# Expert weights of a routed feed-forward layer: rank comparison in 16 bit by quarters, one factor applied on ScalarE, heads summed on GpSimd

## The chip, the cores and the metric

The kernel runs on one core of a Trainium2 chip. The metric is the device time of one execution in microseconds; a kernel is judged by the median of its runs. The engines are named as in the profile: PE (TensorE; PEld is its weight load), DVE (VectorE), ACT (ScalarE), POOL (GpSimd), SP (the queue that issues DMAs).

## The reference, cut to what matters

One transformer layer on `x[8, 512, 256]`: `x + attention(layernorm(x)) + ffn(layernorm(x))`. Attention has 16 heads of width 16 and three branches (compressed, selected blocks, local window). The feed-forward part adds a dense gated layer and a lookup of experts by product keys:

```python
sim = jnp.einsum('btphn,hkpn->pbthk', q, keys)      # p: x or y half, 4 heads, 64 keys
sc, ix = jax.lax.top_k(sim, 8)
all_sc = sc[0][..., :, None] + sc[1][..., None, :]   # 8 x 8 pairs per head
scores, pk = jax.lax.top_k(all_sc.reshape(b, t, 4, 64), 8)
idx = take(ix[0] * 64 + ix[1], pk)                   # expert = x * 64 + y
w = silu(einsum('btd,bthkd->bthk', hidden, down_embed[idx])) * softmax(scores)
experts_states = einsum('bthk,bthkd->btd', w, up_embed[idx])
mlp = silu(h @ Wg + bg) * (h @ Wu + bu) @ Wd + bd
```

There are 1024 experts, so x counts in 16 places (NX = 16) and y in 64 (NK = 64). For every token the kernel needs a dense row of 1024 weights: for each head the softmax weight of a chosen pair (x, y), zero elsewhere, summed over the four heads (PH = 4).

## The kernel before, in words

The 4096 tokens are 32 tiles of 128 tokens (partitions); four tiles make a batch row. For each tile a set of generator functions does one stage each: `queries`, `logits`, `select`, `compressed`, `weights`, `products` and `finish` are attention, `choose_experts`, `route` and `experts` are the product-key lookup, `hidden` (for two tiles at a time) is the dense layer, and `project` multiplies by the up embeddings and the output weights and stores. Nearly all matmuls have f32 operands.

The order on each engine is written at build time by a planner, the class `Conductor`. A stage yields the engine and the buffers that it needs next; the planner keeps a clock for each engine, adds a cost for every recorded instruction (`FIXED` plus `EACH` per element in `book`, with extra terms), and lets the stage go on that can start first, by rank where two are within `NEAR`. Each engine then executes its instructions strictly in that order, waiting on semaphores. So an instruction that is late holds up all that stand behind it on its engine. `Stock` objects are sets of buffers: two pairs of PSUM banks for attention scores (`pairs`), four single banks (`banks`), two 128x1024 f32 buffers (`bigs`), two buffers for exponentiated scores (`wTs`). All instructions are recorded in one helper, so every row of the profile says L160, and rows are told apart by the tensors that they write and read.

The stages around the change:

- `choose_experts` (line 974) takes the top 8 of 64 keys for both halves and four heads, builds one-hot tables in 16 bit (`at_y` in one of the `bigs`, shown as `big<-cbf,ix`, and `at_x`), counts how many y each x keeps, and lets 16 matmuls on the one-hot tables put into one PSUM bank the rank of each y place less 8, and the number of y that each x place keeps. ACT copies these to `rc` (lines 1031 to 1034), head by head. `ed` holds exponentiated scores, 4 heads x (64 + 16), the x part divided by the softmax sum.
- `route` (line 1051) makes the row `gw` of 1024 weights. For each head DVE writes a 0/1 mask of 16 x 64 into a `big` buffer (rank + 8 < count, `big<-rc`), POOL multiplies it by y's factor and then by x's factor from `ed` (`big<-big,ed`), and adds it to `gw` (`gw<-gw,big`; for the first head the second product goes to `gw` itself).
- `experts` (line 1080) multiplies tokens by the down embeddings, applies silu in two steps (ACT writes a tanh to `aT`, DVE combines), transposes `gw` on PE, and multiplies.

The other uses of ACT are copies out of PSUM (`acs`, `qx`, `lg`, `q`, `attnT` and others), exponentials of attention scores (`wT`), and two activations for each of eight steps of `hidden` (`xg`, and one in place in PSUM), which take a bias column by pointer.

Of the kernel before, what the change touches and what calls it, by code (L numbers as in the profile page):

```python
# [9 lines left out]
BF16 = mybir.dt.bfloat16  # L10
U32 = mybir.dt.uint32
AF = mybir.ActivationFunctionType
ALU = mybir.AluOpType
# [3 lines left out]
P = 128  # L17
# [9 lines left out]
NEXP = 1024  # L27
NK = 64
PH = 4
KPH = 8  # L30
NX = NEXP // NK
# [10 lines left out]
_BF_COLS = [  # L42
    ("identb", P), ("win", P + WIN), ("caus", P), ("causT", P), ("bandT", P), ("prevT", WIN),
    ("cmask", NT * NB), ("oneh", 2 * G),
    ("ytab", NK * PH), ("ranks", KPH * P),
]


# [12 lines left out]
def shape_constants():  # L61

    p = np.arange(P)[:, None]
    q = np.arange(P)[None]
    c = np.zeros((P, NCONST), np.float32)
    m = np.zeros((P, NBF), np.float32)

    def put(name, v):
        a, b = _OFF[name]
        c[:, a:b] = v  # L70

    def putb(name, v):
        a, b = _BOFF[name]
        m[:, a:b] = v

    put("ident", np.eye(P))
    put("any", p >= G)
    put("grp", p // 32 == np.arange(4)[None])
    put("head4", p // NB == np.arange(H)[None] % 4)

    putb("identb", np.eye(P))
    back = p + WIN - np.arange(P + WIN)[None]
    putb("win", np.where((back >= 0) & (back <= WIN), 0.0, OUT))
    putb("caus", np.where(q <= p, 0.0, OUT))
    putb("causT", np.where(p <= q, 0.0, OUT))
    putb("bandT", np.where((q - p >= 0) & (q - p <= WIN), 0.0, OUT))
    putb("prevT", np.where(np.arange(WIN)[None] <= p % WIN, 0.0, OUT))

    pos = P * np.arange(NT)[None, :, None] + p[:, :, None]
    n = np.arange(NB)[None, None]  # L90
    low = -(1.0 + n / 128.0) * 2.0 ** 100
    putb("cmask", np.where(pos >= (n + 1) * G, 0.0, low).reshape(P, -1))
    r = np.arange(2 * G)[None]
    putb("oneh", r % G == NT * 2 * (r // G) + p // G)
    putb("ytab", np.arange(NK * PH)[None] // PH)
    putb("ranks", np.concatenate([(j - KPH) * np.eye(P) for j in range(KPH)], 1))
    return c, m.astype(ml_dtypes.bfloat16)


def bc(ap, axis, n):  # L100
    a = ap.unsqueeze(axis)
    shape = list(a.shape)
    shape[axis] = n
    return a.to_broadcast(shape)
# [59 lines left out]
class Conductor:  # L164
# [19 lines left out]
    def book(self, eng, op, args, kw):  # L184
        aps = [a for a in [*args, *kw.values()] if hasattr(a, "shape")]
        n = max(int(np.prod(a.shape[1:])) for a in aps)
        if eng == "PE":
            if op == "transpose":
                cost = 0.11
            else:  # L190
                n = int(np.prod(args[2].shape[1:]))
                cost = (n * 0.42e-3 if args[2].dtype == BF16 else max(n, 32) * 1.68e-3) / self.share
        elif eng == "SP":
            cost = 0.06
        else:
            each = self.EACH[eng]
            if eng == "DVE" and all(a.dtype == BF16 for a in aps):
                each /= 2
            cost = self.FIXED[eng] + each * n
            if op in ("match_replace", "max_index", "tensor_tensor_reduce"):  # L200
                cost += 0.08
        j = self.cur
        start = max(self.at[eng], j.end + (self.HOP[j.eng] if eng != j.eng else 0.0))
        if eng == "POOL" or eng == "DVE" and op in ("tensor_tensor", "scalar_tensor_tensor") and not any(
                a.tensor is self.psum.tensor for a in aps):

            s, e = self.port["DVE" if eng == "POOL" else "POOL"]
            if s <= start:
                start = max(start, e)
            self.port[eng] = (start, start + cost)  # L210
        self.at[eng] = start + cost
        self.busy[eng] += cost
        j.end, j.eng = start + cost, eng
# [41 lines left out]
def tile_kernel(ctx, tc, x, wq, wk, wqT, wv, wo, wck, wcv, wga, bga, wgu, bg, bu, wd, bd,  # L255
# [5 lines left out]
    pe, vec, act, pool, sp = (Engine(con, e, n) for e, n in (  # L261
        (nc.tensor, "PE"), (nc.vector, "DVE"), (nc.scalar, "ACT"), (nc.gpsimd, "POOL"),
        (nc.sync, "SP")))
    mm = pe.matmul
# [3 lines left out]
    def buf(name, shape, dt=F32):  # L268
        return cp.tile(shape, dt, name=name, tag=name)

    def stock(name, n, shape, dt=F32):
        return Stock(con, [buf(f"{name}{i}", shape, dt) for i in range(n)])
# [26 lines left out]
    def const(name):  # L299
        a, b = _OFF[name]  # L300
        return cst[:, a:b]

    def bconst(name, rows=slice(0, P)):
        a, b = _BOFF[name]
        return cbf[rows, a:b]

    ident, identb = const("ident"), bconst("identb")
    cmask = bconst("cmask").rearrange("p (i n) -> p i n", n=NB)
    ytab = bconst("ytab").rearrange("p (y h) -> p y h", h=PH)
# [8 lines left out]
    bigs = stock("big", 2, [P, NEXP])  # L318
# [87 lines left out]
    cnt, et = buf("cnt", [P, KPH, PH], BF16), buf("et", [P, 2 * PH, KPH])  # L406
    past, rz = buf("past", [P, PH, KPH]), buf("rz", [P, PH])
    eds = stock("ed", 2, [P, PH, NK + NX])
    rcs = stock("rc", 2, [P, PH * (NK + NX)])
    lasts = stock("last", 2, [P, 1])  # L410
    gws = stock("gw", 1, [P, NEXP])
    aTs = stock("aT", 2, [P, 8, P])
# [14 lines left out]
    for m in range(2):  # L427
        pfh = banks.take()
        for c in range(4):
            mm(pfh.ap[:, c * P:(c + 1) * P], wpqT_s[:, c, m * P:(m + 1) * P], keys_s[:, c, :],  # L430
               start=True, stop=True)
# [6 lines left out]
    PE, DVE, ACT, POOL, SP = "PE", "DVE", "ACT", "POOL", "SP"  # L438
# [535 lines left out]
    def choose_experts(t):  # L974
# [4 lines left out]
        for kc in range(2):  # L979
            mm(pt.ap, t.row.xnT.ap[:, kc, i * P:(i + 1) * P], wf_s[:, kc, :], start=kc == 0,  # L980
               stop=kc == 1)
# [8 lines left out]
        ed = t.ed.ap  # L990
# [31 lines left out]
        pr = pt.ap[:, :PH * (NK + NX)]  # L1022
        for j in range(KPH):
            rank = bconst("ranks")[:, j * P:(j + 1) * P]
            mm(pr[:, :PH * NK], rank, at_y[:, j].rearrange("p y h -> p (y h)"),
               start=j == 0, stop=False, skip_group_check=True)
        for j in range(KPH):
            mm(pr[:, PH * NK:], identb, at_x[:, j].rearrange("p x h -> p (x h)"),
               start=False, stop=j == KPH - 1, skip_group_check=True)
        ayh.free()  # L1030
        yield ACT,
        for lo, n in ((0, NK), (PH * NK, NX)):
            act.copy(t.rc.ap[:, lo:lo + PH * n].rearrange("p (h y) -> p h y", y=n),
                     pr[:, lo:lo + PH * n].rearrange("p (y h) -> p h y", y=n))
        pt.free()
        yield DVE,
        vec.tensor_tensor(sums, bc(et[:, :PH, :], 3, KPH), bc(et[:, PH:, :], 2, KPH), ALU.mult)
# [13 lines left out]
    def route(t):  # L1051

        yield None, t.ev("r")
        ed = t.ed.ap
        ry = t.rc.ap[:, :PH * NK].rearrange("p (h y) -> p h y", y=NK)
        cx = t.rc.ap[:, PH * NK:].rearrange("p (h x) -> p h x", x=NX)
        for h in range(PH):
            mh = yield DVE, bigs
            m = mh.ap.rearrange("p (x y) -> p x y", y=NK)
            vec.scalar_tensor_tensor(m, bc(ry[:, h, :], 1, NX), float(KPH), bc(cx[:, h, :], 2, NK),  # L1060
                                     ALU.add, ALU.is_lt)
            yield POOL,
            pool.tensor_tensor(m, m, bc(ed[:, h, :NK], 1, NX), ALU.mult)
            exb = bc(ed[:, h, NK:], 2, NK)
            if h == 0:
                t.gw = yield POOL, gws
                g3 = t.gw.ap.rearrange("p (x y) -> p x y", y=NK)
                pool.tensor_tensor(g3, m, exb, ALU.mult)
            else:
                yield POOL,  # L1070
                pool.tensor_tensor(m, m, exb, ALU.mult)
                yield POOL,
                pool.tensor_tensor(g3, g3, m, ALU.add)
            mh.free()
        pool.tensor_tensor(t.gw.ap[:, NEXP - 1:], t.gw.ap[:, NEXP - 1:], t.last.ap, ALU.add)
        for x_ in (t.ed, t.rc, t.last):
            x_.free()
        t.done("gw")
# [112 lines left out]
    for jp in range(2):  # L1191
        each(tiles, lambda t: t.n + 0.24, finish(jp))
    each(tiles, lambda t: t.n + 0.15, choose_experts)
    each(tiles, lambda t: t.n + 0.2, route)
    each(tiles, lambda t: t.n + 0.5, experts)
    each(halves, lambda h: 2 * h.n, fetch)
# [52 lines left out]
```

## Time and profile before

| | |
|---|---|
| median of 3 runs | 1878.66 us (1877.88 to 1882.4) |
| profiled execution | 1871.73 us, span 1869.9 us |
| mean granted TensorE clock | 0.969 |
| PE busy | 1696.6 us, 91% of the span |
| PEld busy | 1271.4 us, 68% |
| DVE busy | 1479.3 us, 79% |
| ACT busy | 692.6 us, 37% |
| POOL busy | 1022.6 us, 55% |
| DMA | 56.11 MB, mean 30 GB/s |

Busy time is the part of the span in which an engine had an instruction in work; a wait for a shared resource within an instruction counts as busy, a wait for a semaphore does not. The chain of waits follows the last instruction back to what released each step; its shares say which engine's work stood one behind the other.

### The profile page before, as it was taken

The numbers are of one execution on the slowest core, as the hardware profiler recorded it, in microseconds if no ns is written. First come the engines' busy times: TensorE is split into PE (matmuls) and PEld (weight loads), VectorE is DVE, ScalarE is ACT, GpSimd is POOL, SyncE is SP. The second block draws the span as 40 slices with busy tenths as digits, with TensorE's granted clock in tenths as the row PEclk, the third lists the DMA queues.
The fourth block names the chain that finished last, engine by engine and source line by source line (L and its number), as shares of the span: only waits on it lengthen the run. The fifth ranks groups of instructions, "written<-read, shape, count | busy, mean of one in ns | idle before, by whom it ended". The sixth has DMA issues, their size and how long they took to land.

```text
span 1869.9 us, 47619 instructions
## 1 busy us (share of the span) xinstructions
PE 1696.6 (91%) x19208; PEld 1271.4 (68%) x19208; DVE 1479.3 (79%) x5292; ACT 692.6 (37%) x1370; POOL 1022.6 (55%) x789
## 2 busy tenths in 40 slices
PE   3899989999989988899899998989989899998989
PEld 2677666777667766677677765766757677676657
DVE  2688896978879789768879878688786877969982
ACT  1353424424345232443334432334324333343233
POOL 2156647454766356556355562755546556474663
PEclk9999989999999999999899999999999999998999
DMA  5011100111001100010000110001000010100000
GB/s 175 10 42 25 30 18 13 36 36 32 24 24 37 25 20 28 24 42 25 18 26 28 42 32 18 13 25 42 25 24 24 20 36 25 30 19 18 30 24 18
DMA packets 55068, 56.11 MB, mean 30 GB/s; under 512 B 21696, under 2 KB 38080, under 8 KB 54848
## 3 DMA queue, kind: packets, MB, share of 16 engines
q1 hardware_dynamic: 54848, 53.07, 9.9%
q8 instruction: 151, 2.47, 0.6%
q14 instruction: 69, 0.57, 0.1%
HBM read 48.02 MB, written 4.19 MB: 28 GB/s over the span
## 4 chain that ended last, share of the span: by engine, by line
PE 61%; DVE 30%; issue 3%; ACT 2%; POOL 1%; SPq 1%; DMA 1%; DVEq 0%; ACTq 0%; POOLq 0%
PE psum L160 61%; DVE bm L160 4%; DVE big L160 3%; DVE mr L160 2%; DVE ixu L160 2%; DVE pick L160 2%; DVE ml L160 1%; DVE aT L160 1%; DVE at_x L160 1%; DVE sums L160 1%; ACT wT L160 1%; DVE top L160 1%; SPq L160 1%; DVE junk L160 1%; DVE hT L160 1%
## 5 line engine op out<-in xcount | busy, mean ns | idle before, releaser
L160 POOL TENSOR_TENSOR big<-big,ed 128x1024 f32<-128x1024 f32 x224 | 488.6, 2181 | 427.5 <-DVE big L160 387.9
L160 ACT ACTIVATE wT<-psum 128x1024 f32<-128x1024 f32 x224 | 219.3, 1023 | 167.4 <-PE psum L160 167.2
L160 PE MATMUL psum<-xnT,wb 128*128 128x256 f32 x1024 | 256.2, 395 | 22.6 <-DVE aT L160 13.7
L160 DVE TENSOR_REDUCE bm<-psum 128x32 f32<-128x512 f32 (+2 forms) x224 | 200.3, 912 | 69.8 <-PE psum L160 69.6
L160 PEld LDWEIGHTS psum<-xnT,wb 128*128 128x128 f32 x1024 | 193.1, 196 | 59.7 <-DVE aT L160 14.5
L160 POOL TENSOR_TENSOR gw<-gw,big 128x1024 f32<-128x1024 f32 x96 | 229.6, 2392 | 6.7
L160 PE MATMUL psum<-k,q 32*128 32x384 f32 (+3 forms) x1024 | 186.5, 469 | 1.6 <-DVE ml L160 1.6
L160 DVE SCALAR_TENSOR_TENSOR big<-rc 128x1024 f32<-128x1024 f32 x128 | 166.2, 1298 | 5.8 <-POOL gw L160 3.7
L160 PE MATMUL psum<-qx,k 32*128 32x128 f32 (+1 forms) x4352 | 152.4, 271 | 11.8 <-DVE ml L160 9.9
L160 PEld LDWEIGHTS psum<-qx,k 32*128 32x128 f32 (+1 forms) x4352 | 125.9, 174 | 48.9 <-issue 29.8
L160 PE MATMUL psum<-wT,v 128*32 128x128 f32 x3584 | 138.7, 280 | 16.6 <-ACT wT L160 15.7
L160 PEld LDWEIGHTS psum<-wT,v 128*32 128x32 f32 x3584 | 87.3, 110 | 80.7 <-ACT wT L160 37.0
L160 PE MATMUL psum<-xnT,deT_s 128*128 128x128 f32 x1024 | 135.5, 289 | 4.3 <-DVE yo L160 1.8
L160 PEld LDWEIGHTS psum<-xnT,deT_s 128*128 128x128 f32 x1024 | 128.6, 203 | 15.0 <-issue 2.7
L160 PE MATMUL psum<-wd_s,hT 128*128 128x256 f32 x512 | 124.8, 389 | 4.9 <-DVE hT L160 4.2
L160 DVE SCALAR_TENSOR_TENSOR aT<-aT,psum 128x512 f32<-128x512 f32 x128 | 87.1, 681 | 49.5 <-ACT aT L160 34.0
L160 ACT ACTIVATE xg<-psum,bgh 128x256 f32<-128x256 f32 x128 | 61.0, 477 | 164.8 <-PE psum L160 164.3
L160 PE MATMUL psum<-ue_s,aT 128*128 128x256 f32 x512 | 119.5, 384 | 2.1 <-DVE aT L160 1.7
L160 PEld LDWEIGHTS psum<-wd_s,hT 128*128 128x128 f32 x512 | 94.9, 193 | 22.5 <-DVE hT L160 5.1
L160 PEld LDWEIGHTS psum<-ue_s,aT 128*128 128x128 f32 x512 | 94.6, 190 | 18.7 <-DVE aT L160 1.9
L160 PEld LDWEIGHTS psum<-k,q 32*128 32x128 f32 x1024 | 76.0, 185 | 42.9 <-issue 32.7
L160 DVE SCALAR_TENSOR_TENSOR xg<-psum,xg 128x256 f32<-128x256 f32 x128 | 53.5, 418 | 59.9 <-ACT psum L160 59.6
(161 smaller groups left out, 3185.2 us busy)
## 6 DMA issues: line engine op xcount, KB each, us to landing
wb<-in_wgu SPq DMA_DIRECT2D x128, 256.0 KB, 2.6
xl<-in_x SPq DMA_DIRECT2D x8, 512.0 KB, 4.0
yo<-in_x SPq DMA_DIRECT2D x32, 128.0 KB, 2.1
out<-yo SPq DMA_DIRECT2D x32, 128.0 KB, 1.7
vl<-v SPq DMA_DIRECT2D x96, 8.5 KB, 1.8
deT_s<-in_deT SPq DMA_DIRECT2D x1, 1024.0 KB, 5.2
wd_s<-in_wd SPq DMA_DIRECT2D x1, 1024.0 KB, 7.7
ue_s<-in_ue SPq DMA_DIRECT2D x1, 1024.0 KB, 10.1
```

Source lines behind the costliest of these rows:

```text
L160: return f(*a, **k)
```

## The change

The masks of the four heads of a tile are no longer made head by head. They are made in four quarters of the x places, each quarter for all heads: 4 x places, 64 y places and 4 heads, again 1024 elements. DVE compares in 16 bit into a new buffer `chosen` (two of them). ACT then multiplies by x's factor: for each head and each x place of the quarter one activation of 64 elements, which takes the factor as its scale by pointer from `ed` and writes f32 to a `big` buffer. POOL multiplies the quarter by y's factor, adds the upper two heads to the lower two (512 elements), and adds the remaining two into the quarter of `gw` (256 elements). `rc` becomes 16 bit and keeps the order of PSUM, so ACT copies it in one piece; the 8 that the comparison used to add is now subtracted from the counts by one more matmul of 64 columns. The planner adds 0.09 to the cost of an activation with a scale or bias by pointer.

```diff
@@ _BF_COLS, shape_constants
-    ("ytab", NK * PH), ("ranks", KPH * P),
+    ("ytab", NK * PH), ("ranks", KPH * P), ("less8", 1),
...
+    putb("less8", -float(KPH))
@@ Conductor.book
+            if op == "activation" and any(hasattr(kw.get(k), "shape") for k in ("scale", "bias")):
+                cost += 0.09
@@ buffers
-    rcs = stock("rc", 2, [P, PH * (NK + NX)])
+    rcs = stock("rc", 2, [P, PH * (NK + NX)], BF16)
+    chosens = stock("chosen", 2, [P, NEXP], BF16)
@@ choose_experts
             mm(pr[:, PH * NK:], identb, at_x[:, j].rearrange("p x h -> p (x h)"),
-               start=False, stop=j == KPH - 1, skip_group_check=True)
+               start=False, stop=False, skip_group_check=True)
+        mm(pr[:, PH * NK:], identb, bconst("less8").to_broadcast([P, PH * NX]),
+           start=False, stop=True, skip_group_check=True)
         ayh.free()
         yield ACT,
-        for lo, n in ((0, NK), (PH * NK, NX)):
-            act.copy(t.rc.ap[:, lo:lo + PH * n].rearrange("p (h y) -> p h y", y=n),
-                     pr[:, lo:lo + PH * n].rearrange("p (y h) -> p h y", y=n))
+        act.copy(t.rc.ap, pr)
@@ route
-        ry = t.rc.ap[:, :PH * NK].rearrange("p (h y) -> p h y", y=NK)
-        cx = t.rc.ap[:, PH * NK:].rearrange("p (h x) -> p h x", x=NX)
-        for h in range(PH):
-            mh = yield DVE, bigs
-            m = mh.ap.rearrange("p (x y) -> p x y", y=NK)
-            vec.scalar_tensor_tensor(m, bc(ry[:, h, :], 1, NX), float(KPH), bc(cx[:, h, :], 2, NK),
-                                     ALU.add, ALU.is_lt)
+        ry = t.rc.ap[:, :PH * NK].rearrange("p (y h) -> p y h", h=PH)
+        cx = t.rc.ap[:, PH * NK:].rearrange("p (x h) -> p x h", h=PH)
+        t.gw = yield None, gws
+        XC = NX // 4
+        for c in range(4):
+            xs = slice(c * XC, (c + 1) * XC)
+            ch = yield DVE, chosens
+            cho = ch.ap.rearrange("p (x y h) -> p x y h", x=XC, h=PH)
+            vec.tensor_tensor(cho, bc(ry, 1, XC), bc(cx[:, xs, :], 2, NK), ALU.is_lt)
+            mh = yield None, bigs
+            m = mh.ap.rearrange("p (h x y) -> p h x y", h=PH, x=XC)
+            for h in range(PH):
+                if h % 2 == 0:
+                    yield ACT,
+                for x_ in range(XC):
+                    act.activation(m[:, h, x_, :], cho[:, x_, :, h], AF.Copy,
+                                   scale=ed[:, h, NK + c * XC + x_:NK + c * XC + x_ + 1])
+            ch.free()
             yield POOL,
-            pool.tensor_tensor(m, m, bc(ed[:, h, :NK], 1, NX), ALU.mult)
-            exb = bc(ed[:, h, NK:], 2, NK)
-            if h == 0:
-                t.gw = yield POOL, gws
-                g3 = t.gw.ap.rearrange("p (x y) -> p x y", y=NK)
-                pool.tensor_tensor(g3, m, exb, ALU.mult)
-            else:
-                yield POOL,
-                pool.tensor_tensor(m, m, exb, ALU.mult)
-                yield POOL,
-                pool.tensor_tensor(g3, g3, m, ALU.add)
+            pool.tensor_tensor(m, m, bc(ed[:, :, :NK], 2, XC), ALU.mult)
+            yield POOL,
+            half_ = m.rearrange("p h x y -> p h (x y)")
+            pool.tensor_tensor(half_[:, :2], half_[:, :2], half_[:, 2:], ALU.add)
+            pool.tensor_tensor(t.gw.ap[:, c * XC * NK:(c + 1) * XC * NK], half_[:, 0], half_[:, 1],
+                               ALU.add)
             mh.free()
```

## The prediction

> **What bounds the kernel now.** I began with the totals of the page and the chain of waits.
>
> ```profile
> PE 1696.6 (91%) x19208; PEld 1271.4 (68%) x19208; DVE 1479.3 (79%) x5292; ACT 692.6 (37%) x1370; POOL 1022.6 (55%) x789
> ...
> PE 61%; DVE 30%; issue 3%; ACT 2%; POOL 1%; SPq 1%; DMA 1%; DVEq 0%; ACTq 0%; POOLq 0%
> PE psum L160 61%; DVE bm L160 4%; DVE big L160 3%; DVE mr L160 2%; DVE ixu L160 2%; DVE pick L160 2%; DVE ml L160 1%; DVE aT L160 1%; DVE at_x L160 1%; DVE sums L160 1%; ACT wT L160 1%; DVE top L160 1%; SPq L160 1%; DVE junk L160 1%; DVE hT L160 1%
> ```
>
> PE is the largest, DVE second, and the end is set by both in turn. POOL, the engine that `route` loads most, holds 1% of the chain: its time matters only through what it does to others. The table of stretches of 25 us shows how the two take turns.
>
> ```profile
> 575.00:600.00 25.00, 23.47 (x325) 17.53 (x325) 23.63 (x111) 16.19 (x28) 17.36 (x12) 1.00 0.16 44
> 825.00:850.00 25.00, 25.00 (x135) 19.17 (x134) 22.79 (x122) 5.88 (x17) 8.16 (x11) 1.00 0.13 34
> 900.00:925.00 25.00, 18.15 (x130) 11.10 (x127) 23.65 (x97) 5.39 (x15) 8.41 (x10) 0.81 0.04 11
> ```
>
> The columns are PE, PEld, DVE, ACT and POOL busy, then the granted clock. From 825 us PE has no gap; from 900 us DVE is busy 23.65 of 25 us, PE idles 7 us and its clock is granted at 0.81. Relief of DVE can pay only in stretches of the second kind. The heaviest ACT stretch, from 575 us, already holds 16.19 us.
>
> A rule bears on how much there is to win. The Trainium skill (Perfetto Trace Analysis, Identifying the Most-Contended Engine) says that matmul busy time is a bad measure of headroom and weight-load busy time a good one. By that, PE at 68% would leave 32%, and freeing DVE could bring hundreds of us. But in the stretch without a PE gap PEld is at 19.17 of 25, 77%. Against that ceiling 68% is 0.89, so 11% is the most, and the totals of PE (91%) say 9%. I go by the trace.
>
> What PE waits for:
>
> ```profile
> PE psum L160 <- DVE aT L160: 24.5, 12, 5.9
> PE psum L160 <- DVE atc L160: 21.8, 10, 6.2
> PE psum L160 <- DVE hT L160: 17.4, 13, 3.1
> PE psum L160 <- ACT wT L160: 15.7, 24, 1.2
> ```
>
> (us in total, times, longest). DVE's waits are few and long, ACT's many and at most 1.2 us: ACT, idle 63% of the time, answers at once. The change touches exactly that.
>
> **DVE.** The removed and the nearest kept comparisons, as minimum/median/maximum in ns:
>
> ```profile
> L160 DVE SCALAR_TENSOR_TENSOR big<-rc x128: 1195/1216/2922, 87.9 to 1831.3; 128x1024 f32<-128x1024 f32 x128
> L160 DVE TENSOR_TENSOR big<-cbf,ix x32: 1212/1226/3247, 71.6 to 1764.7; 128x2048 bf16<-128x2048 bf16 x32
> L160 DVE TENSOR_TENSOR at_x<-cbf,ix x32: 411/420/2584, 72.8 to 1767.0; 128x512 bf16<-128x512 bf16 x32
> ```
>
> The last two have the form of the new comparison: 16 bit, a table repeated along one axis, innermost runs of 4 heads. Their medians give (1226 - 420) / 1536 = 0.525 ns an element, so 420 + 512 x 0.525 = 689 ns for 1024. The old one has a mean of 1298 ns, 82 above its median. How much waiting does the new one get? The skill (SBUF — State Buffer, Who interferes with whom) says that a DVE instruction with two SBUF inputs and a GpSimd instruction that reads SBUF exclude each other, and the later one waits for the whole of the other. Old and new both have two SBUF inputs, but the old one's row shows little of that, since POOL mostly stood waiting for it. The two 16-bit rows do show it: means of 1593 and 804 in the groups by shape, 367 and 384 above their medians. By the old row a new comparison is 771 ns and 128 of them save 67 us; by the rule, as those two rows price it, 1064 ns and 30 us. In the change ACT stands between DVE and POOL, so POOL is no longer idle by design when DVE compares, but its instructions are shorter: I take 250 ns of waiting, 939 ns, 359 saved, 46 us.
>
> POOL's part also frees DVE's other instructions. Mean less median, times 32, over the groups `at_y` (shown as `big<-cbf,ix`), `at_x` (2), `sums` (2), `pick`, `ix`, `et`, `ed`, `xn` is about 91 us of such waiting. The wait of a late comer goes with the square of the length of what it meets. The rows for POOL (busy us, mean ns of one, then idle time before):
>
> ```profile
> L160 POOL TENSOR_TENSOR big<-big,ed 128x1024 f32<-128x1024 f32 x224 | 488.6, 2181 | 427.5 <-DVE big L160 387.9 <-DVE gm L160 15.7 <-PE psum L160 7.2
> L160 POOL TENSOR_TENSOR gw<-gw,big 128x1024 f32<-128x1024 f32 x96 | 229.6, 2392 | 6.7
> ```
>
> A tile now has 7 x 2.18 + 1.99 + 3 x 2.39 = 24.4 us (squares 54); after it has 4 x (2.35 + 1.2 + 0.65) = 16.8 us (squares 30). The 2.35 is the median of `big<-big,ed`; 1.2 for 512 elements lies between half of `gw<-gw,big` and the 1.05 us of `ec`, 0.65 for 256 is near `ext<-mr,ms` (682 ns mean). Squares fall by 46%; with POOL's other work unchanged I take 40% of 91, 36 us; bounds 0 and 50. POOL itself loses 7.6 x 32 = 243 us.
>
> What of this lies on the path? DVE has 30% of 1869.9 = 561 us of its 1479 on the chain, 38%; `big` has 3%, 56 us of the 217 us of its two groups, 26%. So 46 x 0.26 + 36 x 0.38 = 26 us gained. Ends: 30 x 0.26 = 8, and (67 + 50) x 0.38 = 45. POOL's chain share, 19 us of 1023, makes its 243 us worth 4.
>
> **ACT.** 16 activations a quarter, 64 a tile, 2048 in all. None of them is in the trace; the nearest rows:
>
> ```profile
> L160 ACT ACTIVATE et<-et 128x64 f32<-128x64 f32 x32 | 8.2, 257 | 58.7 <-DVE et L160 58.6
> L160 ACT ACTIVATE xg<-psum,bgh 128x256 f32<-128x256 f32 x128 | 61.0, 477 | 164.8 <-PE psum L160 164.3
> ```
>
> ```profile
> 600.90 0.48 ACT L160 ACTIVATE xg<-psum,bgh 128x256 f32<-128x256 f32 x1 [1.14 <-PE psum L160]
> 601.27 0.44 ACT L160 ACTIVATE psum<-psum,bgh 128x256 f32<-128x256 f32 x1
> ...
> 619.44 0.37 ACT L160 COPY vtok<-psum 128x256 f32<-128x256 f32 x1 [0.18 <-PE psum L160]
> 619.71 0.38 ACT L160 COPY v<-psum 128x256 f32<-128x256 f32 x1
> ```
>
> Back to back, an instruction of 256 elements starts 0.37 us after one with a pointer, and 0.27 us after one without: 0.10 us for the pointer. `et` (64 elements, from SBUF) is followed after 0.16 us (618.65 to 618.81). So 0.26 us each: 4.2 us a quarter, 16.6 us a tile, 532 us in all. Ends: 0.16 (the pointer free), 328 us; 0.36 (no overlap), 737 us. The planner books 0.07 + 64 x 0.00083 + 0.09 = 0.213, so each batch of 16 runs 0.75 us longer than the order assumes. The one `rc` copy instead of two saves about 0.15 x 32 = 5 us.
>
> In the built order 112 batches have all 16 back to back and 32 have 8; `wT` stands directly behind 41 batches and `qx` behind 39, both in front of PE's attention matmuls; behind 21 it is `xg`, which feeds DVE. The cover of the batches is ACT's idle time; where PE or DVE needs the copy behind a batch, the cover is gone and up to 4.2 us show. A batch itself waits for a `chosen` and for POOL to free a `big`, and with it waits everything behind it on ACT. ACT's present work is on the chain for 37 of 693 us, 5.4%. At that share 532 us cost 29; for the copies that now come late behind batches I add 11: 40 us. Ends: 328 x 0.054 = 18, and 737 x 0.10 = 74.
>
> **PE** gets 32 matmuls of 64 columns, 0.05 to 0.2 us each by the row of `at_x` (13.3 us busy for 256; 197 ns each), at 61% on the chain 1 to 4 us: 2. No DMA is added; SP keeps its transfers.
>
> **Sum**, against the profiled span of 1869.9: -26 - 4 + 40 + 2 = +12, so 1882. The median of the runs stands 8.8 above the span, so about 1891, slower by 0.6%. Ends: -45 - 5 + 18 + 1 = -31 (1848) and -8 - 3 + 74 + 4 = +67 (1946).
>
> **Rivals.**
>
> *ACT hides, DVE's relief shows (faster).* The place is the stretches like 900 us, where DVE is full and ACT is at 5 of 25 us. If the batches lie there, they cost nearly nothing, about 10 us, and the freed DVE time counts at the mean share: 82 x 0.38 = 31. Then -31 - 4 + 10 = -25, about 1854. It decides where ACT's growth on the chain stays below the 30 us that DVE and POOL give, that is while ACT has less than about 3.6% of the chain. For it: ACT's idle 63%. Against it: the batches follow the comparisons, which are spread over all stretches. 34%.
>
> *ACT becomes the gate of attention (clearly slower).* Scores sit in two pairs of banks until `wT` is out; with 4.2 us in front, PE finds no free pair. If each of the 80 batches ahead of `wT` and `qx` costs 1 us: -30 + 80 + 2 = +52, about 1931. Against it: PE has the dense layer and the experts to go on with. 18%.
>
> *The comparison does not run at 16-bit speed*, so it stays near 1.2 us: DVE's 12 us fall away, +24, about 1903. The `at_x` row speaks against it. 5%.
>
> The small loss of the sum keeps 43%, and it reaches to no change and below. A difference of 0.3%, 5.6 us, is about what a measurement of this kernel can tell from none. From the cases: faster 0.34, within 0.3% 0.13, slower 0.53. The range 1844 to 1950 takes in the ends of the costs and the centres of the rivals.
>
> **What would show it.** DVE busy near 1400 us, POOL near 780, ACT near 1230 with 2048 rows `big<-chosen,ed` of about 0.35 us; `chosen<-rc` at a median of 0.69. If the sum is right, the chain shows ACT at 4 to 5% and DVE below 29%, and PE's waits for `wT` and `qx` rise from 18 us to some 50. I am wrong toward faster if those waits stay, toward slower if they pass 100 us or if ACT idles long before `big` for POOL or DVE.

## The result and the profile after

The change makes the kernel slower: the median went from 1878.27 to 1936.28 us, ratio 1.0336 (95% interval 1.0312 to 1.036). The profiled execution took 1936.62 us with a span of 1934.8 and a mean granted TensorE clock of 0.954, where it was 0.969. The forecast was 1891; its range held the time and its direction was right, but the loss is 58 us and not 12.

Totals and the chain of waits of the changed kernel:

```profile
PE 1742.0 (90%) x19240; PEld 1303.5 (67%) x19240; DVE 1359.9 (70%) x5292; ACT 1163.9 (60%) x3386; POOL 803.9 (42%) x821
...
PE 52%; DVE 28%; ACT 13%; issue 4%; DMA 1%; POOL 0%; SPq 0%; ACTq 0%; DVEq 0%; POOLq 0%
PE psum L161 52%; ACT big L161 7%; DVE bm L161 4%; DVE ixu L161 3%; ACT wT L161 3%; DVE ml L161 2%; DVE top L161 1%; DVE chosen L161 1%; DVE pick L161 1%; DVE mr L161 1%; DVE aT L161 1%; DVE hT L161 1%; DVE big L161 1%; DVE at_x L161 1%; DVE xg L161 1%
```

DVE lost 119 us and POOL 219, and the kernel is still slower: ACT, with 60% the second-least busy engine, went from 2% of the chain to 13%, and 7% is the new rows alone. So an engine with 40% idle time can still be on the path; which of its work is there, and why, the waits below show. The groups of the new instructions (busy us, mean ns of one, idle before and releaser):

```profile
L161 ACT ACTIVATE big<-chosen,ed 128x64 f32<-128x64 bf16 x2048 | 511.5, 341 | 112.9 <-DVE chosen L161 103.7 <-POOL mx L161 5.8 <-POOL gw L161 3.2
L161 POOL TENSOR_TENSOR big<-big,ed 128x1024 f32<-128x1024 f32 x128 | 301.7, 2357 | 611.5 <-ACT big L161 589.3 <-PE psum L161 21.4
L161 POOL TENSOR_TENSOR big<-big 128x512 f32<-128x512 f32 x128 | 168.1, 1314 | 8.2
L161 POOL TENSOR_TENSOR gw<-big 128x256 f32<-128x256 f32 x128 | 105.1, 821 | 10.0
L161 DVE TENSOR_TENSOR chosen<-rc 128x1024 bf16<-128x1024 bf16 x128 | 96.0, 750 | 0.0
```

511.5 / 2048 is 0.25 us from one activation to the next, 4.0 us for 16. POOL now waits for ACT (589 us), as it waited for DVE before. What PE waits for (total, times, longest):

```profile
PE psum L161 <- ACT wT L161: 62.8, 46, 4.2
PE psum L161 <- DVE bm L161: 30.1, 31, 4.3
...
PE psum L161 <- DVE hT L161: 8.7, 9, 3.9
...
PE psum L161 <- ACT qx L161: 7.3, 3, 3.1
...
PE psum L161 <- DVE aT L161: 5.3, 6, 0.9
...
PE psum L161 <- DVE atc L161: 2.3, 1, 2.3
```

DVE's long waits are mostly gone (`aT` 24.5 to 5.3, `atc` 21.8 to 2.3, `hT` 17.4 to 8.7); the wait for `wT` went from 15.7 to 62.8 us. Thirteen of its 46 waits, 35 us in all, last 2.3 to 2.9 us each, and in each the exponential stands behind a batch (in one, a copy of `qx` lies between). The longest, 4.2 us at 113 us, is of another kind: there ACT has finished its batch and waits 3.75 us for DVE in front of `et`, which stands ahead of the exponential. One of the thirteen, first ACT's and then PE's timeline:

```profile
697.41 3.98 ACT L161 ACTIVATE big<-chosen,ed 128x64 f32<-128x64 bf16 x16 [1.07 <-DVE chosen L161]
701.30 1.91 ACT L161 ACTIVATE wT<-psum 128x1024 f32<-128x1024 f32 x2
```

```profile
697.38 1.17 PE L161 MATMUL psum<-qx,k 32*128 32x128 f32 x32
698.49 1.08 PE L161 MATMUL psum<-ecT,vc 128*32 128x128 f32 x32
702.35 0.68 PE L161 MATMUL psum<-wT,v 128*32 128x128 f32 x16 [2.79 <-ACT wT L161]
```

ACT starts a batch at 697.41. PE has written the last scores at 698.55 and has done its other work at 699.57. The exponentials start only at 701.30, when the batch is over; PE stands for 2.79 us until the first of them, 1 us long, is done.

Which matmuls wait for `wT` (the end of the rows is their idle time):

```profile
L161 PE MATMUL psum<-wT,v 128*32 128x128 f32 x3584 | 148.0, 291 | 51.4 <-ACT wT L161 48.0
L161 PE MATMUL psum<-k,q 32*128 32x384 f32 x256 | 61.3, 556 | 14.8 <-ACT wT L161 14.8
```

48.0 of the 62.8 us stand in front of the matmuls that read the exponentials. Only 14.8 us stand in front of matmuls that write new scores and need a free pair of banks.

Of the 65 us by which the span grew, PE's idle time is 19 (1934.8 - 1742.0 against 1869.9 - 1696.6) and PE's busy time 45, for the same matmuls and 32 small ones. Stretches of the changed kernel (PE, PEld, DVE, ACT, POOL busy, then the clock); the last two are the place above and what follows it:

```profile
700.00:725.00 25.00, 21.18 (x226) 13.59 (x226) 16.90 (x52) 8.95 (x24) 6.71 (x9) 0.80 0.03 10
925.00:950.00 25.00, 21.03 (x187) 12.91 (x186) 15.17 (x38) 12.22 (x35) 10.10 (x12) 0.77 0.06 14
697.40:702.30 4.90, 2.17 (x65) 1.78 (x64) 0.00 (x0) 4.89 (x18) 0.77 (x1) 1.00 0.24 57
702.90:709.60 6.70, 6.70 (x38) 3.89 (x36) 4.25 (x11) 2.58 (x6) 3.67 (x6) 0.50 0.00 0
```

In 900 to 925 us of the kernel before, DVE was at 23.65; in the two long stretches here PE idles with no engine full, and the clock is granted at 0.80 and 0.77. The last row shows how PE's busy time grew: after the wait of 2.79 us PE works without a gap, but at half the clock, in a stretch of 6.8 us.

Such a stretch begins during each of the thirteen waits or within 2.8 us after it; these thirteen stretches sum to 92 us. Over the whole execution there are 31 stretches at half clock with 177 us, where the kernel before has 21 with 116 us. If each part of PE's busy time is multiplied by the clock granted in it, the sum is 1649 us before and 1659 after. So about 35 of the 45 us go with the lower clock.

### The profile page after: what moved, and what is told of

The parts are those of the page before. It is cut to its first block, busy times and chain, and to the rows that moved or that the text cites. A ratio compares the mean times of both kernels' runs of the same rounds, so it can differ in the third digit from the quotient of the medians.

```text
span 1934.8 us, 49797 instructions
## 1 busy us (share of the span) xinstructions
PE 1742.0 (90%) x19240; PEld 1303.5 (67%) x19240; DVE 1359.9 (70%) x5292; ACT 1163.9 (60%) x3386; POOL 803.9 (42%) x821
## 4 chain that ended last, share of the span: by engine, by line
PE 52%; DVE 28%; ACT 13%; issue 4%; DMA 1%; POOL 0%; SPq 0%; ACTq 0%; DVEq 0%; POOLq 0%
PE psum L161 52%; ACT big L161 7%; DVE bm L161 4%; DVE ixu L161 3%; ACT wT L161 3%; DVE ml L161 2%; DVE top L161 1%; DVE chosen L161 1%; DVE pick L161 1%; DVE mr L161 1%; DVE aT L161 1%; DVE hT L161 1%; DVE big L161 1%; DVE at_x L161 1%; DVE xg L161 1%
## 5 line engine op out<-in xcount | busy, mean ns | idle before, releaser
L161 ACT ACTIVATE big<-chosen,ed 128x64 f32<-128x64 bf16 x2048 | 511.5, 341 | 112.9 <-DVE chosen L161 103.7
L161 POOL TENSOR_TENSOR big<-big,ed 128x1024 f32<-128x1024 f32 x128 | 301.7, 2357 | 611.5 <-ACT big L161 589.3
L161 PE MATMUL psum<-k,q 32*128 32x384 f32 (+3 forms) x1024 | 197.6, 489 | 14.9 <-ACT wT L161 14.8
L161 PE MATMUL psum<-wT,v 128*32 128x128 f32 x3584 | 148.0, 291 | 51.4 <-ACT wT L161 48.0
L161 PE MATMUL psum<-qx,k 32*128 32x128 f32 (+1 forms) x4352 | 167.7, 278 | 14.2 <-DVE ml L161 8.9
L161 PEld LDWEIGHTS psum<-qx,k 32*128 32x128 f32 (+1 forms) x4352 | 138.6, 180 | 49.4 <-issue 21.8
L161 POOL TENSOR_TENSOR big<-big 128x512 f32<-128x512 f32 x128 | 168.1, 1314 | 8.2
L161 PE MATMUL psum<-cbf 128*128 128x512 bf16 (+3 forms) x376 | 103.6, 349 | 30.1 <-DVE bm L161 30.1
L161 DVE TENSOR_TENSOR yo<-psum,yo 128x256 f32<-128x256 f32 x64 | 26.9, 421 | 128.8 <-PE psum L161 126.8
L161 PEld LDWEIGHTS <-cbf 128*128 128x128 bf16 x888 | 67.5, 99 | 63.6 <-issue 36.4
```

The costliest lines, as they stand in the source:

```text
L161: return f(*a, **k)
```

## The experiments

Theory 1: ACT's batches stand in front of what PE and DVE wait for. Theory 2: the order that the planner makes of the new work, or the longer way DVE to ACT to POOL, is worse in itself. The planner rewrites the order for each kernel, so kernels with the same order tell most.

**a_const_scale**: order unchanged, each activation cheaper.

```diff
-  act.activation(m[:, h, x_, :], cho[:, x_, :, h], AF.Copy, scale=ed[:, h, NK + c * XC + x_:...])
+  act.activation(m[:, h, x_, :], cho[:, x_, :, h], AF.Copy, scale=0.75)   # booked with + 0.09 as before
```

> The changed kernel with its order kept on every engine, but ACT's 2048 activations take a constant scale, not x's factor by pointer (the factor is left out, the planner books them as before). Each should start about 0.16 us after the one before, not 0.25, so a batch of 16 takes some 2.6 us, not 4.0, and ACT loses 180 of 511 us. Theory 1 (time on ACT in front of PE's and DVE's operands is the loss): about a third of the loss against what the other parts gain comes back, 1895 to 1915 us, and PE's waits for wT fall from 63 us to about 40. Theory 2 (the loss comes from the new order of instructions on PE and DVE, not from ACT's time): 1930 to 1940 us, since the order is the same.

Measured: 1888.46 us, 1.0076 (1.0053 to 1.01). The activations take 249 ns and 322.8 us in all, 0.158 us apart. 189 us less on ACT, with the same order on every engine, took 2.6% off the time, about 48 us; PE's wait for `wT` fell from 62.8 to 36.0 us, and its time at half clock from 177 to 140 us. Theory 1 holds, and more came back than I expected. Part of it may have come by way of DVE, whose busy time fell by 39 us (1359.9 to 1320.7) with the same instructions. Like the next two runs, this one leaves out x's factor, so it measures time and is no version of the kernel.

**b_two_wide**: same order on PE, DVE and POOL, ACT nearly relieved.

```diff
-  16 x act.activation(m[:, h, x_, :], cho[:, x_, :, h], AF.Copy, scale=ed[...])
+  2 x activation(m[:, h - 1:h + 1], cho[:, :, :, h - 1:h + 1] reordered, AF.Copy, scale=0.75)   # booked as 16
```

> The changed kernel, same order on PE, DVE and POOL, but each quarter has two activations of 512 elements with a constant scale in place of 16 of 64 (x's factor is left out; the planner still books 16). ACT's part of route falls from 511 us to about 140. Theory 1: nearly all of the loss goes and the gain of the shorter DVE and POOL work shows, 1840 to 1875 us, PE's waits for wT near the 16 us of before. Theory 2: still 1920 to 1940 us, because the order on PE is that of the changed kernel.

Measured: 1893.43 us, 1.0104 (1.0078 to 1.0131). Totals and PE's waits:

```profile
PE 1722.1 (91%) x19240; PEld 1299.7 (69%) x19240; DVE 1323.4 (70%) x5292; ACT 830.5 (44%) x1594; POOL 794.8 (42%) x821
```

```profile
PE psum L161 <- DVE aT L161: 21.1, 6, 3.5
PE psum L161 <- DVE bm L161: 20.6, 19, 4.8
PE psum L161 <- ACT wT L161: 17.9, 29, 2.3
```

PE's wait for `wT` is back near that of before, 17.9 us, and the time is still 1% above it: neither theory's number. 351 us less on ACT gave back 43 us, no more than the 189 us of a_const_scale did, so with the order fixed the loss is not in proportion to ACT's time. ACT is no longer the gate, but PE follows an order written for long batches.

**b2_wide_booked**: the same two wide activations, booked as what they are.

> Two activations of 512 elements a quarter with a constant scale (x's factor left out), as in the run with two wide ones, but now booked by the planner as what they are, so the order is made for them. If the 17 us by which that run stayed above the kernel before came from an order planned around long batches: 1835 to 1860 us. If they come from the quarters or from the step through ACT as such: 1885 to 1900 us again.

Measured: 1834.0 us, 0.9764 (0.9721 to 0.9808).

```profile
PE 1694.2 (92%) x19240; PEld 1265.0 (69%) x19240; DVE 1325.8 (72%) x5292; ACT 832.2 (45%) x1594; POOL 804.9 (44%) x821
...
PE 59%; DVE 30%; ACT 5%; issue 3%; POOL 1%; DMA 1%; SPq 0%; DVEq 0%; ACTq 0%; POOLq 0%
```

Busy DVE, ACT and POOL time is that of b_two_wide to some 10 us; the order differs, and it is worth 3.4% of the time before (59 us between the medians). So an order written around long batches costs time even where the batches are short, and theory 2 has a share in the loss. The run also shows what quarters, 16-bit comparison and sum of heads could give if ACT's part took 159 us instead of 511: 2.4% less than before. It does not show how: without x's factor it is no finished kernel.

**e_booked**: honest booking.

```diff
-                cost += 0.09
+                cost += 0.13 if n == NK else 0.09
```

> The changed kernel with one number of the planner changed: the 64-element activations are booked at 0.253 us, the spacing measured on the chip, not 0.213; all is computed. If the loss comes from batches running 0.65 us longer than planned (PE's order then asks for operands too early): 1890 to 1915 us. If it is ACT's time itself: 1925 to 1940 us, as the order can't remove it.

Measured: 1946.51 us, 1.038 (1.0347 to 1.0412). PE's waits:

```profile
PE psum L161 <- ACT wT L161: 49.7, 41, 4.2
PE psum L161 <- ACT qx L161: 18.6, 17, 4.1
```

The sum of the two, 68 us, is that of the changed kernel (70). The misbooking was not the cause: with true costs the planner only moves the loss.

**f_before_act**, **f2_load_act**: ACT's load alone on the kernel before. First inside `route`, between mask and product:

> The kernel before, its DVE and POOL work untouched, with 64 more activations of 64 elements a tile on ACT, in steps of 8 and with the scale by pointer, booked by the planner like those of the change; they write a buffer that nobody reads. Theory 1: ACT's batches alone cost more than the whole change does, since DVE and POOL give nothing back: 1940 to 1975 us, with PE's waits for wT at 50 us or more. Theory 2: the planner finds room for work that nobody waits for, 1870 to 1900 us.

Measured: 2069.89 us, 1.1044 (1.1012 to 1.1075), far above both numbers. The step inside `route` also lengthens, in the planner's order, the time for which a `big` is held, so this run doesn't measure ACT alone. The second form comes nearer:

```diff
+            t.done(("mask", h))
...
+    def load_act(t):
+        for q in range(4):
+            yield None, t.ev(("mask", q))
+            for k in range(16):
+                if k % 8 == 0:
+                    yield ACT,
+                act.activation(spare[:, k * NK:(k + 1) * NK], <64 of a 16-bit constant>, AF.Copy, scale=const("any"))
+    each(tiles, lambda t: t.n + 0.2, load_act)
```

> The kernel before with 64 more activations of 64 elements a tile, booked, in a stage of its own that only follows the masks of route: route itself, its buffers and its order of requests are as before, nobody waits for the added results. 98 batches of 16 and 57 of 8 stand on ACT. In the first form, where they stood inside route and held its buffers, the time was 2070. Theory 1 (ACT's time in front of PE's and DVE's operands): 1930 to 1970 us, 60 to 90 over the kernel before, with PE's waits for wT at 45 us or more. Theory 2 (the loss comes from a longer route, DVE to ACT to POOL, which holds its buffers and reorders the rest): 1875 to 1900 us.

Measured: 1968.34 us, 1.0485 (1.0453 to 1.0517). The group and PE's wait:

```profile
L160 ACT ACTIVATE spare<-cbf,cst 128x64 f32<-128x64 bf16 x2048 | 513.7, 345 | 0.0
```

```profile
PE psum L160 <- ACT wT L160: 34.8, 42, 3.7
```

514 us of work that nobody waits for, on an engine with 63% idle time, cost 91 us, 18% of their time. That is more than the change loses in all; the change also gains on DVE and POOL. The planner made a new order here too, so the 91 us hold both the batches and that order. Less than expected shows as waits for `wT`; the chain has ACT at 11% and DVE at 31%. PE idles 47 us more than before and is busy 55 us more for the same matmuls, at a mean clock of 0.950.

**c_x_on_pool**: the change without ACT.

```diff
-            (16 activations, then) pool.tensor_tensor(m, m, bc(ed[:, :, :NK], 2, XC), ALU.mult)
+            pool.tensor_tensor(m, cho.rearrange("p x y h -> p h x y"), bc(ed[:, :, :NK], 2, XC), ALU.mult)
+            pool.tensor_tensor(m, m, bc(ed[:, :, NK + c * XC:NK + (c + 1) * XC], 3, NK), ALU.mult)
```

> The changed kernel, but x's factor is applied by POOL in a second multiplication of 1024 elements (all of the result is computed): the comparison in 16 bit by quarters and the sum of heads in two steps stay, ACT has no part in route. POOL has about 2.35 + 1.9 + 1.3 + 0.75 = 6.3 us a quarter, 25 us a tile, as before the change. Theory 1: DVE's saving of 70 us of busy time shows without ACT's cost, 1850 to 1875 us, at or a little below the kernel before. Theory 2 (quarters in place of heads, with their order and their buffers, are worse in themselves): 1890 us or more.

Measured: 1851.58 us, 0.989 (0.9859 to 0.9922), theory 1's number.

```profile
PE 1684.2 (91%) x19240; PEld 1267.3 (69%) x19240; DVE 1412.1 (76%) x5292; ACT 686.7 (37%) x1338; POOL 1044.0 (56%) x949
```

POOL is as busy as before the change and DVE lost 67 us: a gain without any relief of POOL.

**g_f32_mask**: c with the mask written as f32 into `big`.

> The version with x's factor on POOL, but DVE's comparison writes its mask as f32 straight into the big buffer that POOL multiplies in place; inputs stay 16 bit, all is computed. The comparison should take about 1.2 us, not 0.7, 128 times: 65 us more of DVE work. If the 25 us that version gained come from the 16-bit comparison: 1865 to 1885 us, the gain gone. If they come from the sum of heads in two steps and the quarters: 1845 to 1860 us, the gain kept.

Measured: 1912.11 us, 1.0211 (1.0178 to 1.0245), worse than the kernel before. The comparison (minimum, median, maximum in ns):

```profile
L161 DVE TENSOR_TENSOR big<-rc x128: 1885/1944/3397, 88.0 to 1878.2; 128x1024 f32<-128x1024 bf16 x128
```

It takes 1944 ns, not 1.2 us, so the run overshoots its aim: its f32 output goes to elements that lie 1 KB apart, where the old comparison (1216 ns) wrote densely. It still gives a rough price for DVE's time: DVE is busy 137 us more than in c (1549.2 against 1412.1), the time 60 us more, 0.44 us for each. The order and the buffers that DVE asks for differ too. From before to c the price is 0.37 (25 us for 67).

**d_rank_later**: let others go first on ACT.

```diff
-                if h % 2 == 0:
-                    yield ACT,
+                yield ACT,
...
-    each(tiles, lambda t: t.n + 0.2, route)
+    each(tiles, lambda t: t.n + 1.2, route)
```

> The changed kernel with route ranked one tile later and asking for ACT anew every 4 activations, so that attention's exponentials and copies may go first; all is computed. 79 batches of 16 are left of 112, the rest are cut to 4, 8 or 12. Theory 1: PE's waits for wT fall from 63 to some 45 us and the time to 1905 to 1925 us. Theory 2: 1930 to 1950, as nothing is taken from route's length.

Measured: 1995.4 us, 1.0632 (1.0587 to 1.0678), wrong for both theories; PE waits 65.0 us for `wT`, no less, and 11.9 for `gw`, which it had not waited for. A later `route` is itself needed by `experts`. Two things were changed at once, so no more than that follows.

**h_one_quarter**, **i_two_quarters**: part of the x factors on ACT, the rest on POOL as in c (`if c == 0:` and `if c % 2 == 0:` ahead of the activations).

> The version with x's factor on POOL, but for the first of the four quarters ACT applies it with 16 activations of 64 as in the change (512 in all, 128 us of ACT, all is computed); POOL loses a multiplication a tile, 60 us. If ACT's narrow activations cost in proportion to their time (93 us for 2048 when added alone): about 20 us more than x on POOL, less a few for POOL, 1862 to 1878 us. If ACT has room for some of them and only a large share hurts: 1845 to 1855 us.

> As with one quarter on ACT, but two of the four (1024 activations of 64, 256 us; all is computed). Known so far: none 1852 us, one quarter 1830, all four 1936. If ACT's cost goes on the path from the first batch and the gain of one quarter is only an accident of the order: 1860 to 1885 us, on the line between none and four. If ACT has room until batches crowd in front of attention's exponentials: 1825 to 1850 us, at or near the best, and the loss comes with the third and fourth quarter.

Measured: 1830.17 us, 0.9759 (0.9731 to 0.9786) with one quarter, the fastest version that computes everything; 1923.67 us, 1.0241 (1.0191 to 1.0291) with two. With none, one, two and four quarters it is 1852, 1830, 1924 and 1936 us: not in proportion, and both runs fell outside both of their expectations, one below and one above. PE's waits for `wT`, one quarter and then two:

```profile
PE psum L161 <- ACT wT L161: 9.7, 16, 1.2
```

```profile
PE psum L161 <- ACT wT L161: 42.8, 29, 3.5
```

In the built orders no batch stands directly in front of a `wT` with one quarter, and 20 do with two (41 in the changed kernel). The next runs test that with the amount of work held fixed.

**j1_second_quarter**, **j3_fourth_quarter**, **k13_odd_quarters**: the same amounts on other quarters (`c == 1`, `c == 3`, `c % 2`).

> One quarter on ACT as in the fast version, but the second of the four, not the first (512 activations, all is computed). ACT, DVE and POOL have the same amount of work. In the built order 23 of its batches stand directly in front of a wT; with the first quarter it was none, and 1830 us. If the loss comes from batches in front of attention's exponentials: 1850 to 1875 us, PE's waits for wT at 20 us or more. If only the amount of work on ACT counts: 1825 to 1838 us.

> The same with the fourth quarter on ACT; 9 batches stand in front of a wT. Batches in front of exponentials: between the other two, 1835 to 1855 us. Amount of work alone: 1825 to 1838 us. If it lies above the one with 23, neither is the measure, and the order differs by more than what these counts hold.

> Two quarters on ACT, the second and the fourth (1024 activations, all is computed); 35 batches stand in front of a wT, where the version with the first and third has 20 and took 1924 us. Batches in front of exponentials: 1930 to 1960 us. Amount of work alone: 1915 to 1930 us.

| quarters on ACT | batches in front of `wT` | PE waits for `wT`, us | median, us | ratio (interval) |
|---|---|---|---|---|
| first | 0 | 9.7 | 1830.17 | 0.9759 (0.9731 to 0.9786) |
| fourth | 9 | 15.4 | 1867.36 | 0.9945 (0.9925 to 0.9965) |
| second | 23 | 28.3 | 1873.07 | 1.0002 (0.9989 to 1.0015) |
| first, third | 20 | 42.8 | 1923.67 | 1.0241 (1.0191 to 1.0291) |
| second, fourth | 35 | 46.0 | 1940.13 | 1.0357 (1.0332 to 1.0382) |
| all | 41 | 62.8 | 1936.28 | 1.0336 (1.0312 to 1.036) |

The same work on every engine takes 1830 to 1873 us, so the amount on ACT alone is refuted as the measure. Batches in front of `qx`, which the prediction counted too, don't go with the time: in the table's order they are 16, 3, 2, 26, 1 and 39. Within each amount the time rises with the count of those in front of `wT`, but 9 batches cost nearly as much as 23 (1867 us, above what I expected for 9), so that count is no scale either. What else sets apart two orders of equal work, the runs don't tell; with 43 us between the first quarter and the second, a difference of some 20 us between two orders should not be read as the price of one edit.

## Why the prediction was wrong in size

**Right.** The direction, the durations of the new instructions (POOL's small sums ran longer) and who is late next. The comparison: 689 ns forecast, median 682 measured. Activations: 0.26 us apart forecast, 0.25 measured. POOL: 16.8 us a tile forecast, 18.0 measured (4 x (2.36 + 1.31 + 0.82)); busy 804 against 780. PE's waits for `wT` and `qx` together: "some 50" forecast, 70 measured. The second rival, ACT as the gate of attention, gave 1931 at 18% and comes nearest. Its mechanism holds in part: attention does wait for ACT behind batches, but mostly for the exponentials themselves (48.0 us) and not for a free pair of banks (14.8 us), and the clock, which it doesn't name, carries much of the loss. That its number fits to 5 us is luck. Luck had a part in the direction too: the sum stood at +12, and its two largest terms were off by some 50 and 20 us, in opposite directions.

**Wrong: ACT's share of the path.** The step that failed is "At that share 532 us cost 29". The 5.4% was the share of the copies and exponentials of the kernel before, which came singly, about half a microsecond long, on an engine that was idle two thirds of the time. I priced batches of 4 us at the share of single instructions and added 11 us for what stands behind them. Alone on the kernel before they cost 91 us (f2_load_act, its new order included), 18%. In the order of the change, 189 us less of ACT's time gave back 48 us (a_const_scale), 25%, and 351 us less gave back 43 (b_two_wide), 12%. The term was 40 us; 91 is the one direct measurement of it, and the share is no constant.

**Wrong: DVE's worth.** Here too I was low, in the other direction. The old row's waiting was the right guide and the rule's price, as I read it off the 16-bit rows, was not: the mean of 750 ns is 68 above the median, where I took 250. The comparisons save 70 us, not 46, and DVE as a whole 119, not 82. I counted the comparisons at 26% on the path; 137 us of DVE time cost 60 in g_f32_mask, 44%. With 38% to 44% of 119 us, DVE's gain is 45 to 52 us, where I had 26. The balance then is -45 to -52, -4 for POOL, +91 and +2: +37 to +44, against 58 measured (1.0336). What remains, 14 to 21 us, is within what two orders of equal work differ by (43 us between the first and the second quarter), so the balance doesn't prove its terms.

**Wrong: "Ends: ... 737 x 0.10 = 74".** Even the upper bound of ACT's term was below the measured price, since I doubled the share only as far as 10%; only the second rival, added by hand, held it.

**Left out: the clock and the order.** I showed a stretch with PE idle and a clock of 0.81 and did not put it into the sum. I also gave PE's waits over 100 us as the sign of a larger loss. They reached 70, and the loss was larger all the same, because PE's busy time grew by 45 us. In all sixteen traces PE's busy time, multiplied by the clock granted in it, stays between 1647 and 1666 us, while the busy time itself goes from 1684 (c_x_on_pool) to 1788 (f_before_act). By these traces a wait of PE that brings a half-clock stretch costs more than its own length. No run changed the clock alone, so this rests on what follows what in the traces. And I took the order as given: b_two_wide against b2_wide_booked shows that an order made for long batches costs 3.4% even without them. What it costs in the changed kernel itself stays open, since true bookings (e_booked) did not help.

**Two readings of the kernel before.** The heaviest stretch for ACT is not that from 575 us but that from 100 us, with 16.64 us. And 77% is no ceiling for PEld: from 1425 us PE is busy 25.00 of 25 us too, with PEld at 21.44, 86%. Neither entered the sum.

## What to carry to other kernels

An engine's idle share says how much work fits in, not what it costs: ask for how long the new work holds the engine at a time, and what stands behind it in the queue. Before splitting an elementwise step into many narrow instructions on the engine that empties PSUM, put the same load there as a dummy and look at the waits of TensorE; 514 us of useless activations at 63% idle cost 91 us here. Where a planner writes the order, judge an edit by several orders of the same work, and try part of it: one quarter on ScalarE and three on GpSimd was 2.4% faster than the kernel before when it was the first, 0.5% faster as the fourth and no faster as the second; all four were 3.4% slower. And count a wait of TensorE together with the clock granted after it.

## What the runs showed of the hardware

A scale by pointer adds 92 ns to an activation of 64 elements (341 ns mean in the changed kernel against 249 in a_const_scale, 0.25 against 0.158 us apart). On GpSimd a product of 1024 f32 elements takes a median of 2357 ns with both operands varying along the innermost axis (changed kernel), 1902 where the factor is repeated along it, and 2411 with one operand in 16 bit and 8-byte steps (both c_x_on_pool). VectorE's comparison of 1024 elements from 16-bit inputs takes a median of 682 ns with a dense 16-bit output (changed kernel) and 1944 ns with an f32 output whose innermost step is 1 KB (g_f32_mask).

The clock's records of these traces hold full and half clock and nothing between; the half-clock stretches of the changed kernel last 3.4, 6.8 or 10.2 us. Of PE's 25 waits of over 2 us in the changed kernel, 22 had such a stretch begin during the wait or within 4 us of its end; of the 106 waits of 0.3 to 1 us, 14 did. In b2_wide_booked it was 3 of 8 of the long waits, so the length of a wait alone doesn't decide it.
